# Middle elements: group statistics over DRAM in place of two small matmuls, and another order of VectorE's and ScalarE's work between the attentions

## The chip, the cores and the metric

The kernel runs on one core of one Trainium2 chip. The metric is the device time of one execution in microseconds, the median of several runs. The engines of the core have names that the text uses: TensorE (PE in the profile, its weight loads PEld) multiplies matrices into PSUM; VectorE (DVE) and ScalarE (ACT) work on SBUF and empty PSUM; GpSimd (POOL) does small things and issues some DMAs; SyncE (SP) issues most of the DMAs. Each engine works through its own queue in order.

## The reference

Two layers on x of shape (16, 256, 32, 32), in float32. With S = 1024 positions and C = 256 channels, for each of the 16 elements of the batch:

```python
# layer 0
qkv = (xs @ w_proj + b_proj).reshape(B, S, 4, 192); q, k, v = split(qkv)
attn = softmax(einsum('bihd,bjhd->bijh', q, k) * 64**-0.5, axis=2)
x = einsum('bijh,bjhd->bihd', attn, v) @ w_out + b_out + xs

# layer 1
x = x + attention(group_norm(x, gn1_w, gn1_b), qkv_w, proj_w, proj_b, phys_bias)  # 8 heads of 32
h = group_norm(x, gn2_w, gn2_b)                                                   # 32 groups of 8 channels
h = gelu(mlp_w1 @ h + mlp_b1, approximate=False)                                  # 256 -> 1024
return x + mlp_w2 @ h + mlp_b2
```

`group_norm` takes mean and variance over the 8 channels of a group and all positions, and then `(x - mean) / sqrt(var + 1e-5) * w + b`.

## The kernel before

**Tiles.** Channels lie on the 128 partitions, in two halves (`cc`); positions lie in two blocks of 512 (`t`). The two attentions keep their scores transposed: keys on partitions, 512 queries along the row. "Attention a" is that of layer 0 (4 heads of 64), "attention b" that of layer 1 (8 heads of 32). Denominators are summed on VectorE (`es`), and their reciprocals go over DRAM and back to all partitions that need them (`sp`, `row`, `d_a`, `rd_b`).

**Stages.** A loop runs over the 16 elements. For element b: attention a; then a middle stage; then attention b, into which the second half of the MLP of the element before is laced; the first half of that MLP (`hidden`: `begin`, `middle`, `finish` of four blocks i = 0 to 3) is in the middle stage. "Middle elements" are 1 to 14 (`seven` is true): there the middle stage holds, in this order on TensorE,

- the MLP's first matrix for element b - 1, as one level of Strassen's scheme: seven products per block, gathered in PSUM tiles `m`. `finish(i)` has VectorE read two PSUM halves (L1265, L1266), ScalarE apply gelu to two quarters (`gelu`, L1224), and VectorE take two differences of gelu'd quarters (`combine`, L1285);
- q and k of attention a for element b + 1, then q and k of attention b for element b, each as Winograd's seven products (`qk_by_seven`, L1096). A piece "a20" is product 2, half 0, for attention a; "b40" is product 4, half 0, for attention b. Products 1, 2, 3, 5, 6 of a half share a PSUM tile `qk_a` or `qk_b` of two banks, products 7 and 4 use the bank `qk7y`. ScalarE copies intermediate states away (L1132, L1137, L1141) and takes k out (L1116, L1118); VectorE takes q out (`leave_q`, L1122 for b, L1124 for a);
- before them VectorE makes four sums and differences of the input (`input_sums`, L1088 to L1091, tile `qk7t`), t1 to t4.

**The norm between the attentions** (`group_norm` with key `g`). `means` (L894) gets mean and variance of each channel (`mv_g`) from statistics that the output projection of attention a leaves. The mean over the eight channels of a group is then a matmul of a 128x2 operand with a constant matrix `gavg` (`averages`, tile `gm_g`), a second one gives the variance (`gv_g`); between and after them VectorE works on 128x2 tiles, GpSimd takes the power of -0.5 (L916), and four `tensor_scalar` of 128x512 (L928) write the normed tile `gn_g`.

**What sets the order.** The program is written in the order of TensorE; a scheduler keeps each engine's instructions near it. `Later` holds what is due so many pieces from now: `later.after(n, fn)`. `tc.issue_after(ins)` gives what is issued inside it a place behind the instruction `ins`, and `tc.keep_in_program_order` pins one. Before, the norm's steps are due 2 and 1 pieces after the statistics, and `input_sums` for attention b stands behind the last `finish`'s VectorE instruction (`mlp_made["added"]`), while gelus and differences stand where `finish` issues them. SP's queue carries in this stage, in this order: the reciprocals of attention a (L405, L422, L427), the load of the second MLP weights (L315) and, in the next stage, the packing of `es_b`.

PSUM is handed out in three tiles of two banks (`wide`, by least recent use) and two single banks (`bank`). A product of `qk_by_seven` that opens a tile therefore waits for the readers of what was in it; a11 opens the one that holds block 2 of the MLP before.

Of the kernel before, what the change touches and what calls it, by code (L numbers as in the profile page):

```python
# [283 lines left out]
def first_pass(ctx, tc, x, out, k):  # L284
    nc = Engines(tc)
    B, C, S = x.shape
    CC, SB, NT = C // P, S // P, S // TB
    HC = k["m1b"].shape[1]
    later = Later()

    act = ctx.enter_context(tc.tile_pool(name="act", bufs=1))
# [574 lines left out]
        return issue  # L866


    def group_norm(key, src, stats, gw, gb, tag, out_tile, wait, then=None):
        st = {}  # L870

        def averages(name, src, apart):
            if cols[0] == P:
                ps = bank(name, 1)
                product(ps[:, :CC], k["gavg"], src, start=True, stop=True)
                return [(slice(0, P), ps[:, :CC])]
            if apart:
                ps = [bank(f"{name}_{n}", n) for n in range(2)]  # L880
            else:
                both = wide(name)
                ps = [both[:, n, :] for n in range(2)]
            halves = [slice(h, h + HALF) for h in range(0, P, HALF)]
            for n, sl in enumerate(halves):
                nc.tensor.matmul(
                    ps[n][sl, :CC], k["gavg"][sl, sl], src[sl], start=True, stop=True
                )
            return [(sl, ps[n][sl, :CC]) for n, sl in enumerate(halves)]

        def means():
            mv = small.tile([P, CC, 2], F32, tag="mv", name=f"mv_{key}")
            for cc in range(CC):
                nc.vector.bn_aggr(mv[:, cc, :], stats[:, cc].rearrange("p t k -> p (t k)"))  # L894
            mean_c = small.tile([P, CC], F32, tag="mean_c", name=f"mean_c_{key}")
            nc.vector.tensor_copy(mean_c, mv[:, :, 0])
            st.update(mv=mv, mean_c=mean_c)
            later.after(wait, variances)

        def variances():  # L900
            mean = small.tile([P, CC], F32, tag="mean", name=f"mean_{key}")
            for sl, ps in averages(f"gm_{key}", st["mean_c"], True):
                nc.vector.tensor_copy(mean[sl], ps)

            dv = small.tile([P, CC], F32, tag="dv", name=f"dv_{key}")
            nc.vector.tensor_sub(dv, st["mean_c"], mean)
            nc.vector.tensor_mul(dv, dv, dv)
            nc.vector.tensor_add(dv, dv, st["mv"][:, :, 1])
            st.update(mean=mean, tv=dv)
            later.after(1 if cols[0] == P else 5, apply)  # L910

        def apply():
            rstd = small.tile([P, CC], F32, tag="rstd", name=f"rstd_{key}")
            for sl, ps in averages(f"gv_{key}", st["tv"], False):
                nc.vector.tensor_scalar(rstd[sl], ps, EPS, None, ALU.add)
            nc.gpsimd.tensor_tensor(rstd, rstd, k["mhalf"], ALU.pow)  # L916
            a = rstd
            nc.vector.tensor_mul(a, rstd, gw)
            ma = small.tile([P, CC], F32, tag="gma", name=f"gma_{key}")
            nc.vector.tensor_mul(ma, st["mean"], a)  # L920
            c = ma
            nc.vector.tensor_sub(c, gb, ma)
            y = act.tile([P, CC, S], F32, tag=tag, name=f"gn_{key}")
            out_tile.append(y)

            def part(cc, t):
                sl = slice(t * TB, (t + 1) * TB)
                nc.vector.tensor_scalar(  # L928
                    y[:, cc, sl], src[:, cc, sl],
                    a[:, cc : cc + 1], c[:, cc : cc + 1], ALU.mult, ALU.add,  # L930
                )

            if nc.in_order:
                then(y, part)
                return
            for t in range(NT):
                for cc in range(CC):
                    part(cc, t)
            if then:
                then(y)  # L940

        means()
# [140 lines left out]
    def input_sums(key, y):  # L1083
        sums = weights_tile(f"qk7t_{key}")
        b11, b12 = (y[:, 0, t * TB : (t + 1) * TB] for t in range(NT))
        b21, b22 = (y[:, 1, t * TB : (t + 1) * TB] for t in range(NT))
        t1, t2, t3, t4 = (sums[:, n] for n in range(4))
        nc.vector.tensor_sub(t3, b22, b12)  # L1088
        nc.vector.tensor_sub(t1, b12, b11)
        nc.vector.tensor_sub(t2, b22, t1)  # L1090
        nc.vector.tensor_sub(t4, b21, t2)  # L1091
        return dict(t1=t1, t2=t2, t3=t3, t4=t4, b11=b11, b21=b21, b22=b22)

    made_k = []

    def qk_by_seven(key, block, s, x, q, kk, bias=None):  # L1096
        ps, ys, got = {}, {}, []

        def aside_for():
            if not got:  # L1100
                got.append(weights_tile(f"qk7p_{key}"))
            return got[0]
# [17 lines left out]
        def leave_q(to, what, more, ch):  # L1120
            if bias is None:
                nc.vector.tensor_add(to, more, what)  # L1122
            else:
                nc.vector.scalar_tensor_tensor(  # L1124
                    to, what, bias[:, 0, ch : ch + 1], more, ALU.add, ALU.add
                )

        def p1(ch):
            both = wide(f"qk7_{key}_{ch}", order[1] if ch == 0 and bias is not None else None)
# [8 lines left out]

        def p6(ch):
            mm(ps[ch][1], s[:, ch, 1], "t2", False)  # L1140
            nc.scalar.copy(aside_for()[:, 2 * ch + 1], ps[ch][1])  # L1141

        def p2(ch):
            mm(ps[ch][0], block(1, ch, 1), "b21", False)
# [52 lines left out]
    def mlp(b, xb):  # L1197
# [61 lines left out]
        def finish(i):  # L1259
            if i == n4 - 1 and b == B - 2:  # L1260
                later.after(1, back_to_exp)
            ps = open_sums.pop(i)
            products_of(i, [(7, ps[:, 0, :], False), (6, ps[:, 1, :], False)])
            rest = gs[1, 1, i]
            nc.vector.tensor_add(unit(0, 0, i), rest, ps[:, 0, :])  # L1265
            made["added"] = nc.vector.tensor_add(rest, rest, ps[:, 1, :])  # L1266
            gelu(0, 0, i, gs[0, 0, i])
            gelu(1, 1, i, rest)
            combine((1, 0), (0, 0), False, i)
            combine((0, 1), (1, 1), False, i)  # L1270

        def back_to_exp():
            one = small.tile([P, 1], F32, tag="part", name=f"one_{b}")
# [8 lines left out]
        def combine(to, what, plus, only=None):  # L1282
            d, more = ((four if only is None else gs)[(*g, *(() if only is None else (only,)))]
                       for g in (to, what))
            (nc.vector.tensor_add if plus else nc.vector.tensor_sub)(d, d, more)  # L1285
# [179 lines left out]
    for b in range(B):  # L1465
        def load_next(b=b):
# [8 lines left out]
        later.after(14, load_next)  # L1475
        xn = []
        seven = 0 < b < B - 1
        xn_made = []
        run(
            attention_0(  # L1480
                b, tiles0, xs[b],
                lambda st, b=b, xn=xn, seven=seven, xn_made=xn_made: group_norm(
                    f"g{b}", xs[b], st, k["g1w"], k["g1b"], "res", xn, 2 if b else 1,
                    xn_made.append if seven else None,
                ),
            )
        )
# [4 lines left out]
        if seven:  # L1492
            run_pieces(hidden[:1])
            qk_parts = load_qk_blocks(b)
            run_pieces(hidden[1:2])
            with tc.issue_after(mlp_made["begun"].ins):
                sums_0 = input_sums(f"a{b}", xs[b + 1])
            made = {"a": qk_by_seven(
                f"a{b}", qk_block_0, qk_parts[:, 0], sums_0, *tiles0[:2], k["bqk"]
            )}  # L1500
            run_pieces(hidden[2:8] + [made["a"][7, 1]] + hidden[8:])
            first = first_v
        else:
            run_pieces(first[:5] if b == 0 else hidden)
# [9 lines left out]

        if seven:
            with tc.issue_after(mlp_made["added"].ins):
                sums_1 = input_sums(f"b{b}", xn_made[0])
            made["b"] = qk_by_seven(
                f"b{b}", qk_block_1, qk_parts[:, 1], sums_1, *tiles1[:2]
            )  # L1520

            def pieces(names):
                return [made[n[0]][int(n[1]), int(n[2])] for n in names.split()]

            run_pieces(pieces(
                "a10 a70 a11 a60 a40 a61 a50 a41 a51 a20 b10 a21 a30 b60 a31 b11 b70"
                " b50 b61 b71 b20"
            ))
            with tc.issue_after(made_k[-1].ins):
                mlp_made["exp"]()  # L1530
            run_pieces(pieces("b51 b40 b30 b21 b41") + v[:1] + pieces("b31"))
        else:
            aside.extend((1, 0))
            run_pieces(qk[:n] + v[:1])
# [346 lines left out]
```

## Time and profile before

| what | value |
|---|---|
| median of 3 runs | 3586.73 us (3586.65 to 3588.13) |
| the profiled execution's own time | 3587.91 us |
| its span, first to last instruction | 3586.1 us |
| mean granted TensorE clock | 1.000 |
| TensorE busy | 3573.3 us |
| VectorE busy | 2785.1 us |
| ScalarE busy | 2288.7 us |
| GpSimd busy | 220.1 us |
| middle stage of element 2, TensorE, first MLP product to first score | 494.17 to 548.30 us |
| gm_g, gv_g: matmul records in all, mean | 32 and 32, 209 and 213 ns |

A float32 matmul leaves two records in this profile. Records of TensorE overlap and their ends are modelled, so their starts are what counts. In a line of the timeline the columns are start in us from the span's start, duration, engine, line of the kernel, operation, result<-operands, shape, and how many were merged; a bracket gives the idle time ahead of it and who ended it.

### The profile page before, as it was taken

What the parts mean: (1) busy time and instruction counts of PE and PEld (TensorE: products, weight loads), DVE (VectorE), ACT (ScalarE), POOL (GpSimd) and SP (SyncE); (2) the same over time, 40 slices, a digit from 0 to 9 for tenths busy, and PEclk for the clock granted to TensorE, in tenths of its full rate; (3) what the DMA queues carried; (4) which work ended last, traced back from release to release, by engine and by line L of the source; (5) the groups of instructions that cost most, each with busy time, mean ns of one, the idle gap of its engine ahead of it and who ended that gap; (6) DMA issues with size and microseconds to landing.
All of it is one profiled execution on the core that took longest, in us unless ns stands there. A gap on an engine that the chain in (4) does not pass through costs nothing.

```text
span 3586.1 us, 82054 instructions
## 1 busy us (share of the span) xinstructions
PE 3573.3 (100%) x35713; PEld 1479.0 (41%) x35713; DVE 2785.1 (78%) x3188; ACT 2288.7 (64%) x3186; POOL 220.1 (6%) x319
## 2 busy tenths in 40 slices
PE   9999999999999999999999999999999999999999
PEld 4334344343444434444344443444434444344434
DVE  5786877868788687886868878688786877869787
ACT  5665757567575675856658566585765757657573
POOL 4000000001000010000000000000000100000000
PEclk9999999999999999999999999999999999999999
DMA  4011312213122131221312213121121211213100
GB/s 134 8 58 33 82 51 40 72 39 82 45 44 68 39 82 45 52 65 35 82 45 52 66 34 81 45 55 63 39 77 45 55 63 43 72 45 64 52 28 28
DMA packets 81606, 198.07 MB, mean 55 GB/s; under 512 B 38006, under 2 KB 38774, under 8 KB 75094
## 3 DMA queue, kind: packets, MB, share of 16 engines
q1 hardware_dynamic: 71860, 164.13, 15.0%
q0 software_dynamic: 7632, 28.21, 5.1%
q8 instruction: 282, 4.62, 0.5%
q14 instruction: 86, 0.70, 0.1%
q10 hardware_dynamic: 1746, 0.40, 0.1%
HBM read 125.59 MB, written 22.27 MB: 41 GB/s over the span
## 4 chain that ended last, share of the span: by engine, by line
PE 93%; DVE 4%; DMA 1%; issue 1%; SPq 0%; ACT 0%; DVEq 0%
PE s_b L642 13%; PE s_a L458 13%; PE acc_a L481 12%; PE acc_b L696 12%; PE m L1209 9%; PE m L381 9%; PE qk_a L1108 3%; PE qk_b L1108 3%; PE v_b L381 3%; PE j L381 3%; PE v_a L381 3%; PE o L381 3%; PE qk7y_b L1108 1%; PE qk7y_a L1108 1%; DVE es_b L670 1%
## 5 line engine op out<-in xcount | busy, mean ns | idle before, releaser
L655 ACT ACTIVATE e_b<-s_b 128x1024 f32<-128x1024 f32 (+1 forms) x1280 | 982.1, 864 | 135.3 <-PE s_b L642 135.3
L670 DVE TENSOR_TENSOR es_b<-es_b,e_b 128x2048 f32<-128x2048 f32 (+1 forms) x460 | 881.5, 1934 | 105.0 <-ACT e_b L655 88.6
L468 ACT ACTIVATE e_a<-s_a 128x1024 f32<-128x1024 f32 x512 | 521.2, 1025 | 359.1 <-PE s_a L458 356.3
L458 PE MATMUL s_a<-q,k 64*64 64x512 f32 x4096 | 544.3, 593 | 0.0
L481 PE MATMUL acc_a<-e_a,v 64*64 64x512 f32 x4096 | 540.1, 589 | 0.0
L642 PE MATMUL s_b<-q,k 32*64 32x512 f32 x8192 | 523.4, 600 | 2.7 <-ACT v L978 1.3
L495 DVE TENSOR_TENSOR es_a<-es_a,e_a 128x1024 f32<-128x1024 f32 x384 | 471.8, 1229 | 63.7 <-ACT e_a L468 42.9
L696 PE MATMUL acc_b<-e_b,v 128*32 128x512 f32 x4096 | 492.1, 598 | 0.0
L381 PE MATMUL m<-g,w 128*32 128x256 f32 (+1 forms) x6432 | 401.8, 384 | 0.0
L381 PEld LDWEIGHTS m<-g,w 128*32 128x32 f32 x6432 | 218.7, 111 | 205.0 <-issue 54.8
L481 PEld LDWEIGHTS acc_a<-e_a,v 64*64 64x64 f32 x4096 | 187.9, 133 | 251.5 <-issue 222.9
L642 PEld LDWEIGHTS s_b<-q,k 32*64 32x64 f32 x8192 | 175.8, 130 | 247.5 <-issue 122.4
L458 PEld LDWEIGHTS s_a<-q,k 64*64 64x64 f32 x4096 | 175.8, 133 | 247.0 <-issue 216.5
L696 PEld LDWEIGHTS acc_b<-e_b,v 128*32 128x32 f32 x4096 | 108.5, 109 | 351.5 <-ACT e_b L655 194.7
L1209 PE MATMUL m<-gn_h,w 128*128 128x512 f32 x504 | 238.3, 601 | 0.7 <-DVE g L1237 0.7
L670 DVE TENSOR_TENSOR es_b<-e_b,e_b 128x2048 f32<-128x2048 f32 (+1 forms) x72 | 147.0, 2051 | 105.8 <-ACT e_b L655 105.8
L1285 DVE TENSOR_TENSOR g<-g,g 128x512 f32<-128x512 f32 (+1 forms) x184 | 193.5, 1062 | 2.1 <-PE m L381 0.8
L1209 PE MATMUL m<-hs,w 128*128 128x512 f32 x380 | 176.0, 592 | 0.0
L1224 ACT ACTIVATE g<-g,m1b 128x512 f32<-128x512 f32 x128 | 91.6, 721 | 94.1 <-DVE g L1265 67.2
L1209 PEld LDWEIGHTS m<-gn_h,w 128*128 128x128 f32 x504 | 91.8, 190 | 113.9 <-issue 99.1
L1122 DVE TENSOR_TENSOR q<-qk7p_b,qk_b 128x512 f32<-128x512 f32 x28 | 19.3, 688 | 134.5 <-PE qk_b L1108 134.5
L1224 ACT ACTIVATE g<-m,m1b 128x512 f32<-128x512 f32 x128 | 81.0, 684 | 66.8 <-PE m L1209 66.8
(251 smaller groups left out, 3667.6 us busy)
## 6 DMA issues: line engine op xcount, KB each, us to landing
w<-w_kept SPq DMA_DIRECT2D x30, 1792.0 KB
packed_b<-es_b SPq DMA_DIRECT2D x42, 512.0 KB
packed_b<-es_b POOLq DMA_DIRECT2D x42, 512.0 KB, 6.3
rd_b<-row_b SPq DMA_DIRECT2D x252, 64.0 KB
out_dram<-x SPq DMA_DIRECT2D x63, 256.0 KB
d_a<-row_a SPq DMA_DIRECT2D x62, 256.0 KB
x<-in_x_dram SPq DMA_DIRECT2D x30, 512.0 KB
qk<-qk_kept SPq DMA_DIRECT2D x14, 1024.0 KB
```

The costliest lines, as they stand in the source:

```text
L381: nc.tensor.matmul(o[sl], w[:, sl], r, **flags)
L458: nc.tensor.matmul(s[h : h + HALF, g, :], kT[g * D : (g + 1) * D, c, kb * P + h : kb * P + h + HALF], qT[g * D : (g + 1) * D, c, t * TB : ...
L468: nc.scalar.activation(e, s, AF.Exp, scale=float(D) ** -0.5)
L481: nc.tensor.matmul(accs[i][h][g * D : (g + 1) * D, :], v[h * HALF : (h + 1) * HALF, kb, c * 2 + g], e[h * HALF : (h + 1) * HALF, g, :], st ...
L495: spread_out["es"] = nc.vector.tensor_add(sums[i], held[i] if kb == 1 else sums[i], e)
L642: nc.tensor.matmul(outs[g][h : h + HALF, :], kT[g * D : (g + 1) * D, c, k0 : k0 + HALF], qT[g * D : (g + 1) * D, c, t * TB : (t + 1) * TB] ...
L655: spread_out["exp"] = nc.scalar.activation(to, s, AF.Exp, scale=float(D) ** -0.5)
L670: ins = nc.vector.tensor_add(d, (d if kb else es[0][:, g : g + step]), es[m][:, g : g + step])
L696: nc.tensor.matmul(acc[g * D : (g + 1) * D, :], v[:, kb + m, c * G + g], es[m][:, g, :], start=(m == 0), stop=(m == 1),)
L1108: ins = nc.tensor.matmul(to, w, x[right], start=first, stop=True, skip_group_check=not first)
L1209: nc.tensor.matmul(ps, blocks[1][number - 1][:, i * P : (i + 1) * P], inputs[b][number], start=first, stop=True, skip_group_check=not first,)
L1285: (nc.vector.tensor_add if plus else nc.vector.tensor_sub)(d, d, more)
```

## The change

For the middle elements alone:

- The norm's averages over a group no longer come from matmuls. `mv_g` (128 partitions x 4 numbers) is written to a DRAM tile by one DMA, and a second one reads it back so that every partition has the values of all eight channels of its group (tile `of_g`, 128 x 32). `from_group` then does on VectorE: the sum of the means, their distances from the mean, squares, the variances added, the sum, and the division by eight with EPS added. It is due four pieces after the statistics.
- What both ways share after that is now `scale_by` (power, coefficients).
- The four `tensor_scalar` that write `gn_g` become a function, `all_parts`, which the main loop calls after the last `finish`, together with the input sums.
- For blocks 2 and 3 of the MLP the gelus of `finish` and the two differences are kept in lists. The gelus are issued behind ScalarE's copy of a61 (`made_got[-1]`), the differences behind VectorE's last q of attention a (`made_q[-1]`).
- t4 of the input sums is a function of its own (`sums_4`): for a it is issued at once as before, for b after the differences.

TensorE's order stays as it was except for the two matmuls that go. On VectorE, from the end of `begin`: before, coefficients, four gn, then the PSUM readers of block 2 and 3 mixed with differences, sums and the q of a; after, coefficients, the four PSUM readers, four gn, three sums, four q of a, four differences, t4.

```diff
@@ group_norm
             for cc in range(CC):
                 nc.vector.bn_aggr(mv[:, cc, :], stats[:, cc].rearrange("p t k -> p (t k)"))
+            if over_memory:
+                return around(mv)
...
+        def around(mv):
+            row = dram.tile([P // GSZ, GSZ * CC * 2], F32, tag="stats", name=f"row_{key}", bufs=2)
+            nc.sync.dma_start(row.rearrange("g (j f) -> (g j) f", j=GSZ), mv)
+            n = GSZ * CC
+            full = work.tile([P, TB], F32, tag="full", name=f"of_{key}", bufs=2)
+            nc.sync.dma_start(
+                full[:, : 2 * n], row.unsqueeze(1).to_broadcast([P // GSZ, GSZ, 2 * n])
+            )
+            later.after(wait, lambda: from_group(
+                full[:, : 2 * n].rearrange("p (j c f) -> p f c j", c=CC, f=2),
+                full[:, 2 * n : 3 * n].rearrange("p (c j) -> p c j", c=CC),
+            ))
+
+        def from_group(of_group, dv):
+            means, variances = of_group[:, 0], of_group[:, 1]
+            mean = small.tile([P, CC], F32, tag="mean", name=f"mean_{key}")
+            tc.keep_in_program_order(nc.vector.tensor_reduce(mean, means, AX.X, ALU.add))
+            nc.vector.scalar_tensor_tensor(
+                dv, mean.unsqueeze(2).to_broadcast([P, CC, GSZ]), -1.0 / GSZ, means,
+                ALU.mult, ALU.add,
+            )
+            nc.vector.tensor_mul(dv, dv, dv)
+            nc.vector.tensor_add(dv, dv, variances)
+            rstd = small.tile([P, CC], F32, tag="rstd", name=f"rstd_{key}")
+            nc.vector.tensor_reduce(rstd, dv, AX.X, ALU.add)
+            nc.vector.tensor_scalar(rstd, rstd, 1.0 / GSZ, EPS, ALU.mult, ALU.add)
+            st.update(mean=mean)
+            scale_by(rstd, 1.0 / GSZ)
...
-            for t in range(NT):
-                for cc in range(CC):
-                    part(cc, t)
+            if over_memory:
+                mlp_made["norm"] = all_parts
+                return
+            all_parts()
@@ input_sums
-        nc.vector.tensor_sub(t4, b21, t2)
+        sums_4[key] = lambda: nc.vector.tensor_sub(t4, b21, t2)
@@ finish
-            gelu(0, 0, i, gs[0, 0, i])
-            gelu(1, 1, i, rest)
-            combine((1, 0), (0, 0), False, i)
-            combine((0, 1), (1, 1), False, i)
+            steps = (
+                lambda: gelu(0, 0, i, gs[0, 0, i]),
+                lambda: gelu(1, 1, i, rest),
+                lambda: combine((1, 0), (0, 0), False, i),
+                lambda: combine((0, 1), (1, 1), False, i),
+            )
+            if 2 * i >= n4 and b + 2 < B:
+                for what, fn in zip(("gelus", "gelus", "sums", "sums"), steps):
+                    made.setdefault(what, []).append(fn)
+                return
+            for fn in steps:
+                fn()
@@ the main loop
-                    f"g{b}", xs[b], st, k["g1w"], k["g1b"], "res", xn, 2 if b else 1,
-                    xn_made.append if seven else None,
+                    f"g{b}", xs[b], st, k["g1w"], k["g1b"], "res", xn,
+                    4 if seven else 2 if b else 1, None, seven,
...
             with tc.issue_after(mlp_made["added"].ins):
-                sums_1 = input_sums(f"b{b}", xn_made[0])
+                mlp_made.pop("norm")()
+                sums_1 = input_sums(f"b{b}", xn[0])
...
-            run_pieces(pieces(
-                "a10 a70 a11 a60 a40 a61 a50 a41 a51 a20 b10 a21 a30 b60 a31 b11 b70"
-                " b50 b61 b71 b20"
-            ))
+            run_pieces(pieces("a10 a70 a11 a60 a40 a61 a50 a41 a51"))
+            with tc.issue_after(made_got[-1].ins):
+                for fn in mlp_made.pop("gelus"):
+                    fn()
+            with tc.issue_after(made_q[-1].ins):
+                for fn in mlp_made.pop("sums"):
+                    fn()
+                sums_4[f"b{b}"]()
+            run_pieces(pieces("a20 b10 a21 a30 b60 a31 b11 b70 b50 b61 b71 b20"))
```

More of the change, by code (lines that the diff above doesn't have):

```diff
@@ L288, in first_pass @@
     HC = k["m1b"].shape[1]
+    GSZ = C // GROUPS
     later = Later()
@@ L866, in out_proj, with group_norm @@
         return issue
-    def group_norm(key, src, stats, gw, gb, tag, out_tile, wait, then=None):
+    def group_norm(
+        key, src, stats, gw, gb, tag, out_tile, wait, then=None, over_memory=False
+    ):
         st = {}
@@ L915, in apply, with scale_by @@
                 nc.vector.tensor_scalar(rstd[sl], ps, EPS, None, ALU.add)
+            scale_by(rstd, None)
+        def scale_by(rstd, share):
             nc.gpsimd.tensor_tensor(rstd, rstd, k["mhalf"], ALU.pow)
@@ L919, in apply @@
             ma = small.tile([P, CC], F32, tag="gma", name=f"gma_{key}")
-            nc.vector.tensor_mul(ma, st["mean"], a)
+            if share is None:
+                nc.vector.tensor_mul(ma, st["mean"], a)
+            else:
+                nc.vector.scalar_tensor_tensor(ma, st["mean"], share, a, ALU.mult, ALU.mult)
             c = ma
@@ L924, in apply, with all_parts @@
             out_tile.append(y)
+            def all_parts():
+                for t in range(NT):
+                    for cc in range(CC):
+                        part(cc, t)
             def part(cc, t):
@@ L1090, in input_sums @@
         nc.vector.tensor_sub(t2, b22, t1)
-        nc.vector.tensor_sub(t4, b21, t2)
+        sums_4[key] = lambda: nc.vector.tensor_sub(t4, b21, t2)
         return dict(t1=t1, t2=t2, t3=t3, t4=t4, b11=b11, b21=b21, b22=b22)
-    made_k = []
+    made_k, made_q, made_got, sums_4 = [], [], [], {}
     def qk_by_seven(key, block, s, x, q, kk, bias=None):
@@ L1123, in leave_q @@
             else:
-                nc.vector.scalar_tensor_tensor(
+                made_q.append(nc.vector.scalar_tensor_tensor(
                     to, what, bias[:, 0, ch : ch + 1], more, ALU.add, ALU.add
-                )
+                ))
         def p1(ch):
@@ L1140, in p6 @@
             mm(ps[ch][1], s[:, ch, 1], "t2", False)
-            nc.scalar.copy(aside_for()[:, 2 * ch + 1], ps[ch][1])
+            made_got.append(nc.scalar.copy(aside_for()[:, 2 * ch + 1], ps[ch][1]))
         def p2(ch):
@@ L1477, in first_pass @@
         seven = 0 < b < B - 1
-        xn_made = []
         run(
@@ L1481, in first_pass @@
                 b, tiles0, xs[b],
-                lambda st, b=b, xn=xn, seven=seven, xn_made=xn_made: group_norm(
-                    f"g{b}", xs[b], st, k["g1w"], k["g1b"], "res", xn, 2 if b else 1,
-                    xn_made.append if seven else None,
+                lambda st, b=b, xn=xn, seven=seven: group_norm(
+                    f"g{b}", xs[b], st, k["g1w"], k["g1b"], "res", xn,
+                    4 if seven else 2 if b else 1, None, seven,
                 ),
@@ L1497, in first_pass @@
                 sums_0 = input_sums(f"a{b}", xs[b + 1])
+                sums_4[f"a{b}"]()
             made = {"a": qk_by_seven(
```

## The prediction

> **What bounds the kernel now.** I read the page first: busy shares, then the chain that ended last.
>
> ```profile
> PE 3573.3 (100%) x35713; PEld 1479.0 (41%) x35713; DVE 2785.1 (78%) x3188; ACT 2288.7 (64%) x3186; POOL 220.1 (6%) x319
> ...
> PE 93%; DVE 4%; DMA 1%; issue 1%; SPq 0%; ACT 0%; DVEq 0%
> ```
>
> TensorE has no idle time to speak of, and 93% of the chain is its own. But the ends of its records are modelled, so a small stall does not show as idle; it shows in the distance from one start to the next. So I went to the timeline of TensorE in the middle stage (the MLP and the making of q and k between the two attentions) of element 2:
>
> ```profile
> 514.87 1.02 PE L1209 MATMUL m<-gn_h,w 128*128 128x512 f32 x2
> 515.73 0.28 PE L381 MATMUL gm_g<-mean_c_g,gavg 128*128 128x2 f32 x2
> 515.87 1.10 PE L1209 MATMUL m<-gn_h,w 128*128 128x512 f32 x2
> 516.81 1.02 PE L1209 MATMUL m<-hs,w 128*128 128x512 f32 x2
> 517.67 0.28 PE L381 MATMUL gv_g<-dv_g,gavg 128*128 128x2 f32 x2
> 517.81 1.96 PE L1209 MATMUL m<-gn_h,w 128*128 128x512 f32 x4
> 519.61 3.60 PE L1209 MATMUL m<-hs,w 128*128 128x512 f32 x8
> ...
> 529.91 1.02 PE L1108 MATMUL qk_a<-qk7t_a,qk 128*128 128x512 f32 x2
> 530.93 1.12 PE L1108 MATMUL qk_a<-x,wp 128*128 128x512 f32 x2
> ```
>
> The pitch is to be seen: a 128x512 matmul leaves two records, and eight records from 519.61 take until 523.04, 0.429 us each. Nearly everything here starts on that pitch, so the stage is bound by TensorE, and a gain is only what breaks the pitch. Three places do, in all fourteen middle elements, alike to 0.01 us: the two matmuls of the norm, and the first product a20, which starts 1.02 us after its predecessor where two records need 0.86. Who ends that last wait is in VectorE's timeline:
>
> ```profile
> 513.53 0.20 DVE L894 BATCH_NORM_AGGREGATE mv_g<-st 128x2 f32<-128x12 f32 x1
> ...
> 517.87 0.69 DVE L1242 TENSOR_TENSOR g<-g,m 128x512 f32<-128x512 f32 x1 [1.08 <-PE m L1209]
> 518.48 0.15 DVE L915 TENSOR_SCALAR rstd_g<-gv_g 128x2 f32<-128x2 f32 x1
> 519.44 0.16 DVE L918 TENSOR_TENSOR rstd_g<-rstd_g,g1w 128x2 f32<-128x2 f32 x1 [0.81 <-POOL rstd_g L916]
> ...
> 530.13 0.75 DVE L1124 SCALAR_TENSOR_TENSOR q<-qk_a,bqk,qk7p_a 128x512 f32<-128x512 f32 x1
> ```
>
> The second L1124 ends at 530.88, a20 starts at 530.93: its PSUM tile is being read. VectorE had been busy without a break since 519.44 with gn, the MLP's differences and sums.
>
> **The change, part by part.**
>
> *The two matmuls go.* gm: 515.73 to 515.87 is 0.14 us, and the pair after it takes 0.94 to the next start instead of 0.86: 0.08 more, 0.22 together. gv: 0.14, and the four after it take 1.80 instead of 1.716: 0.22. Sum 0.45 us per element, all on TensorE's path; 14 x 0.448 = 6.3 us. They also go from a70's bank, which is then free early; a70 waited for nothing that I see.
>
> *VectorE's small work.* Removed: five 128x2 operations (L896, L903, L906 to L908) and L915, 0.2 us apart. Added: two reductions, three 128x16 operations and a 128x2 one. No 128x16 arithmetic with a broadcast is in the trace; its ends are 0.16 us (128x2) and 0.29 (the one reduction of 128x128 to 128x16). I take 0.25, the 128x16 reciprocal (0.246), and 0.28 with the gap. The chain to the end of the coefficients: 5 x 0.28 = 1.40, from L942 to the answer of GpSimd's power 0.96 (518.48 to 519.44), three small ones 0.59; 2.95 us.
>
> *The two DMAs.* Both go on SP's queue, the second waiting there for the first to land. Behind it on SP stands only the load of the second MLP weights, which before is issued at 523.24, once TensorE has left the first ones; it moves with TensorE. Nothing else of SP's comes before 574. POOL's queue keeps its order. The nearest rows are the reciprocals' way through DRAM:
>
> ```profile
> 498.49 0.32 SPq L422 DMA_DIRECT2D row_a<-inv_a  x1
> 499.89 1.10 SPq L427 DMA_DIRECT2D d_a<-row_a  x2
> ```
>
> ```profile
> 493.24 0.58 SPq L405 DMA_DIRECT2D sp_a<-d_a  x1
> ```
>
> ```profile
> 495.22 0.22 POOL L423 TENSOR_TENSOR dsum<-dsum,sp_a 128x16 f32<-128x16 f32 x1 [25.15 <-DMA sp_a<-d_a]
> ```
>
> A row of 128 small packets is in DRAM and the next issue starts 1.40 us later (1.41 to 1.55 in 26 of 32; 3.1 to 3.5 in six). A gather of 128 small packets reaches its user after 2.0 us (495.22 less 493.24). mv_g ends at 513.73, SP starts 0.04 later: 513.77 + 1.46 + 2.00 = 517.23. Against this speaks the Trainium skill, "DMA: Bandwidth & Descriptors", section "Anatomy of one DMA — SWDGE (gpsimd) path": each DMA has about 2.0 us of fixed cost, mostly the wait for the receipt of its last write, worst where HBM is the target. It is given for GpSimd's path; by it two in a row land at 517.8, estimated, not 517.2. On SP's queue here the write to DRAM is the shorter of the two, so on that point the rows differ from the page and decide. Before TensorE's shift VectorE reaches this point at 518.5: L1242 then starts at 517.87 - 0.22 = 517.65 and is followed 0.6 later, at 518.25. By row and by rule the trip is covered and the sum is the same; I take the row. The ends of the trip's price on the path are nothing and, for an access that crawls, what the third rival gives.
>
> *The order on VectorE.* From 518.25: coefficients until 521.20; then the four PSUM readers of `finish` (0.72 and 0.60 apart): 521.20, 521.92, 522.52, 523.24, so until 523.84. TensorE delivers them no later: its eighth record of `finish` ends, shifted by 0.45, at 522.8. The reader that frees the tile of a11 ends at 522.6, a11 starts at 524.76 - 0.45 = 524.3. Then four gn (1.83, as 520.03 to 521.86) until 525.67, three sums (0.60, 0.72, 0.60) until 527.59, first q until 528.25. The second q needs a50, whose last record (528.62, 0.59 long) ends shifted at 528.76: q runs 528.8 to 529.55. a20 is due at 529.91 + 0.86 - 0.45 = 530.32. So its wait goes: 0.16, and the 0.10 by which its two records are stretched after it (1.12 us where a pair takes 1.02). 0.267 x 14 = 3.7 us. Spare: 0.55 ahead of q, 0.73 behind it. With the landing's 1.02 ahead of 518.25, the trip may take 5.7 us instead of 3.46; even the slow six fit (the longest, 3.51 in place of 1.46, gives 5.5).
>
> *ScalarE.* The four gelus leave the place ahead of the copies for a60 and a61 (nothing waited; price 0) and stand behind a61's copy, which ends near 528.5; 4 x 0.65 bring them to 531.2. Behind them waits the first k, due when a20 ends at 530.32 + 0.43 + 0.59 = 531.3. Were the gelus later, a30 would wait, which is due 2.6 us after a20's start and needs only k's 0.69: 0.9 spare. The four differences and the last sum (t4 of b) come after the fourth q, about 531.3, and end near 534.7, in the hole of VectorE ahead of L1122 at 539.03 (6.84 us of waiting there); b40, which needs t4, is later. If that hole were closed they would cost 3.3 us.
>
> *What is late next.* In the stage after this TensorE keeps its pitch too: 91.34 us busy of the 91.70 us from 548.3 to 640, with VectorE at 75.57 and ScalarE at 74.07. So the shift should carry to the end.
>
> **The sum.** 14 x (0.448 + 0.267) = 10.0 us. The profiled execution took 3587.91 us, its span 3586.1 and 1.8 around it: 3577.9. The median of the runs is 1.18 us lower, 3586.73, so 3576.7 us, 0.28% faster.
>
> **The rivals.**
>
> *Only the matmuls pay.* If the operations with broadcast or the four readers take 1.3 us more than I have it, the second q is late again and a20 waits as before: 6.3 us, 3580.4. For it: every operation there was put at a mean. Against it: 1.28 us of spare.
>
> *It doesn't do what it says.* The shift is taken back later, at the weights or in the attention over memory: 3586.7. For it: VectorE is 82% busy there. Against it: TensorE's own 91.34 of 91.70; and the weights, issued in element 1 at 301.48, are first wanted at 341.2.
>
> *A wait in place of the one removed; slower.* VectorE is in order and now stands for a DMA ahead of the PSUM readers and gn. The point from which it decides: trip over 5.7 us, stall begins; over 6.3 the 0.715 are gone (a stall also stretches by 0.10); beyond 6.8 it is slower by over 0.2%. The same page, "Latency and other measured facts", has HBM's access at 0.2 us on average and 2 us at high load; 1.8 more on top of the 2.0 for each of the two, an estimate, gives 7.6: stall 1.9 + 0.1, less 0.715, times 14 is 18 us: 3605. Against it: the DMA queues are busy 7% from 494.2 to 523.0, and none of the 32 writes took over 3.51 us, no gather over 2.67.
>
> **How the numbers follow.** All of it, 3576.7: 0.70. Only the matmuls: 0.12. Given back: 0.08. The late trip: 0.10. What moves each is where the slow trips of the reciprocals fall: in three of the fourteen elements of before the stage took 1.0 to 1.5 us more (57.3, 57.7 and 57.1 us instead of 56.2, 3.6 in all), and where they fall may change. None of them gives 3573.1, two more give 3579.1: 3573 to 3579.4 for the likeliest alone. With the second case the range is 3573 to 3583, which leaves out 0.18. A measurement of this kernel tells a change from none at about 0.2%, 7.2 us: faster 0.68, within 0.22 (second and third case, and 0.02 of the first), slower 0.10.
>
> **What would show it.** Right: no gm and gv in the middle; the pair at 515.87 at 0.429 pitch; a20 0.86 after its predecessor; VectorE waiting under 0.2 us for the DMA of the group's values; ScalarE's first k not behind a gelu. Wrong: VectorE idle before the first reduction, a11 or a20 off the pitch, or a middle stage shorter by 0.7 us with the same time per element.

## The result and the profile after

| | before | after |
|---|---|---|
| median of 10 runs each | 3586.84 us (3586.51 to 3588.43) | 3577.36 us (3575.98 to 3579.74) |
| profiled execution, its span | 3587.91, 3586.1 us | 3575.98, 3574.2 us |
| middle stage where no row was slow, first to last | 56.16 us (11 of 14) | 55.45 us (11 of 14) |
| middle stage in the other three | 57.30, 57.68, 57.14 us | 56.55, 56.60, 56.64 us |

The ratio is 0.9973, with a 95% interval of 0.9964 to 0.9982: 0.27% faster, where 0.28% and 3576.7 us were predicted. The stage is measured here from the start of TensorE's last denominator record of attention a to the start of its first score of attention b. A "slow row" is one write of the reciprocals of attention a's last half to DRAM (tile `row_a`) that takes about 3 us instead of 1.5; it is shown below. Where there is none, the stage became 0.71 us shorter. The sum over all fourteen stages fell by 10.2 us, from 789.9 to 779.7. The pair of profiled executions differs by 11.9 us; the 1.7 left over lie outside the middle stages and are less than runs of one kernel differ among themselves (3.8 us over ten runs of after). The medians differ by 9.5.

The page of the changed kernel, busy shares and the chain that ended last:

```profile
PE 3561.2 (100%) x35657; PEld 1473.9 (41%) x35657; DVE 2793.3 (78%) x3188; ACT 2285.7 (64%) x3186; POOL 220.5 (6%) x319
...
PE 96%; DVE 2%; DMA 1%; issue 0%; ACT 0%; SPq 0%; DVEq 0%
```

TensorE has 56 records fewer, two matmuls of two records in each of 14 elements. VectorE is 8.2 us busier, and yet its share of the chain fell from 4% to 2%.

The timeline of TensorE in the middle stage of element 2:

```profile
513.23 1.88 PE L1255 MATMUL m<-gn_h,w 128*128 128x512 f32 x4
514.95 1.02 PE L1255 MATMUL m<-hs,w 128*128 128x512 f32 x2
515.80 1.88 PE L1255 MATMUL m<-gn_h,w 128*128 128x512 f32 x4
...
527.82 1.02 PE L1154 MATMUL qk_a<-qk7t_a,qk 128*128 128x512 f32 x2
528.68 1.02 PE L1154 MATMUL qk_a<-x,wp 128*128 128x512 f32 x2
```

The MLP's products follow each other at 0.429 us a record (four from 513.23 to 514.95 are 1.72 us), with nothing between them. a20, the last line, starts 0.86 us after its predecessor, and its pair takes 1.02 us again instead of 1.12.

VectorE's timeline of the same element, from its wait for the last sum of the MLP's second product:

```profile
516.00 0.69 DVE L1288 TENSOR_TENSOR g<-g,m 128x512 f32<-128x512 f32 x1 [1.52 <-PE m L1255]
516.61 0.17 DVE L933 TENSOR_REDUCE mean_g<-of_g 128x2 f32<-128x16 f32 x1
516.82 0.19 DVE L934 SCALAR_TENSOR_TENSOR of_g<-mean_g,of_g 128x16 f32<-128x16 f32 x1
...
518.65 0.16 DVE L955 TENSOR_TENSOR rstd_g<-rstd_g,g1w 128x2 f32<-128x2 f32 x1 [0.81 <-POOL rstd_g L953]
...
519.44 0.69 DVE L1311 TENSOR_TENSOR g<-g,m 128x512 f32<-128x512 f32 x1 [0.23 <-PE m L1255]
...
527.16 0.75 DVE L1170 SCALAR_TENSOR_TENSOR q<-qk_a,bqk,qk7p_a 128x512 f32<-128x512 f32 x1 [0.31 <-PE qk_a L1154]
...
529.55 2.49 DVE L1339 TENSOR_TENSOR g<-g,g 128x512 f32<-128x512 f32 x4
```

L933 is the first operation that needs the gathered statistics; no bracket stands behind it, so they had landed. The first PSUM reader (L1311) and the second q (L1170) now wait for TensorE, where before the second L1124 came too late for a20. That q ends at 527.91, 0.77 us ahead of a20. SyncE's two issues and ScalarE's work ahead of a30, same element:

```profile
512.12 0.33 SPq L919 DMA_DIRECT2D row_g<-mv_g  x1
513.53 0.55 SPq L922 DMA_DIRECT2D of_g<-row_g  x1
```

```profile
526.78 2.56 ACT L1270 ACTIVATE g<-g,m1b 128x512 f32<-128x512 f32 x4
529.74 0.69 ACT L1164 ACTIVATE k<-qk_a,bqk 128x512 f32<-128x512 f32 x1 [0.39 <-PE qk_a L1154]
```

The write is in DRAM 1.41 us after its issue began, when the gather can be issued. The first k waits for TensorE and not behind the four gelus.

The three elements whose stage is longer (1, 6 and 11; before 1, 7 and 13) have one slow write of the reciprocals of attention a. In the changed kernel's element 1, the issues on SyncE's queue, TensorE's starts that break the pitch because of it, and the DMA packets between the two issues (packets, MB, share of 16 engines):

```profile
274.83 0.32 SPq L423 DMA_DIRECT2D row_a<-inv_a  x1
278.08 1.11 SPq L428 DMA_DIRECT2D d_a<-row_a  x2
```

```profile
284.05 3.70 PE L382 MATMUL o<-res_a,wo 128*128 128x512 f32 x8 [0.39 <-DVE res_a L575]
...
292.21 1.98 PE L1255 MATMUL m<-gn_h,w 128*128 128x512 f32 x4 [0.17 <-DVE g L1283]
```

```profile
q1 hardware_dynamic: 144, 0.01, 3.0%
q8 instruction: 1, 0.02, 2.2%
```

The write takes 3.25 us where most take 1.4 to 1.6. Beside its 128 packets of 64 bytes (the other 16 have 4 bytes) there is one packet of 16 KB of the instruction queue, 1.19 us long, that starts just ahead of them; 120 of the 128 had ended by 275.86, and the last eight start only when it ends and have ended at 276.89. Elements 6 and 11 (writes of 3.41 and 3.29 us) show the same, again with exactly eight, which is one engine's share if the 128 are spread evenly over 16. In after and in before alike, all six of the 32 such writes that take over 2 us have a 16 KB packet in their time and eight late packets, and none of the other 26 has. The late packets do not explain all of it: from a write's last packet to the next issue it is 0.4 to 0.7 us in the quick ones, and 1.19 here. Where those 0.5 to 0.8 us more come from stays open.

### The profile page after: what moved, and what is told of

Same layout as the page of the kernel before. It is cut to its first block, busy times and chain, and to the rows that moved or that the text cites. A ratio compares the mean times of both kernels' runs of the same rounds, so it can differ in the third digit from the quotient of the medians.

```text
span 3574.2 us, 81969 instructions
## 1 busy us (share of the span) xinstructions
PE 3561.2 (100%) x35657; PEld 1473.9 (41%) x35657; DVE 2793.3 (78%) x3188; ACT 2285.7 (64%) x3186; POOL 220.5 (6%) x319
## 4 chain that ended last, share of the span: by engine, by line
PE 96%; DVE 2%; DMA 1%; issue 0%; ACT 0%; SPq 0%; DVEq 0%
PE s_b L643 14%; PE acc_b L697 13%; PE s_a L459 12%; PE acc_a L482 12%; PE m L382 10%; PE m L1255 9%; PE qk_b L1154 3%; PE qk_a L1154 3%; PE v_a L382 3%; PE v_b L382 3%; PE j L382 3%; PE o L382 3%; PE qk7y_b L1154 1%; PE qk7y_a L1154 1%; PE qk_a L382 1%; PE den_a L551 1%
## 5 line engine op out<-in xcount | busy, mean ns | idle before, releaser
L382 PE MATMUL v_a<-wp,x 128*32 128x256 f32 (+1 forms) x1952 | 121.6, 379 | 0.0
L382 PE MATMUL o<-res_a,wo 128*32 128x512 f32 (+1 forms) x640 | 118.8, 595 | 1.3 <-DVE res_a L575 1.3
```

The costliest lines, as they stand in the source:

```text
L382: nc.tensor.matmul(o[sl], w[:, sl], r, **flags)
```

## Experiments

All kernels here compute the whole reference. Where there is a ratio, the runs of the kernel before on the same chip stand beside it; otherwise one execution was made, and it is read by its stages.

### The new order alone

The norm goes by its two matmuls as before; the rest of the change stays.

```diff
-            if over_memory:
-                return around(mv)
...
-                    4 if seven else 2 if b else 1, None, seven,
+                    2 if b else 1, None, seven,
```

> The changed kernel with the old norm: the two matmuls are back, the new order of VectorE and ScalarE stays. If the parts pay as in the prediction's sum, the a20 wait stays away and gm and gv cost their 0.45 us: middle stage 0.27 us shorter than before in undisturbed elements (56.16 to 55.90), 3.7 us in all, about 3583. Rival, the order pays nothing by itself: a20 waits again (0.16 us off the pitch), stage 56.16, 3586.8.

Measured: 3583.96 us (3582.53 to 3585.31) against 3587.82, ratio 0.9989 (0.9979 to 0.9999). The stage without a slow row is 55.90 us in all eleven elements: 0.26 less than before and 0.45 more than after. TensorE's timeline of element 2 has the two matmuls and the stretched pair back, and a20 is on the pitch:

```profile
516.24 0.28 PE L382 MATMUL gm_g<-mean_c_g,gavg 128*128 128x2 f32 x2
516.38 1.10 PE L1253 MATMUL m<-gn_h,w 128*128 128x512 f32 x2
517.33 1.02 PE L1253 MATMUL m<-hs,w 128*128 128x512 f32 x2
```

So with the old norm the order is worth a20's wait (0.26 measured, 0.267 predicted) and nothing else, and in this order the two matmuls are worth 0.45 (0.448): both halves of the prediction's sum are what they were put at.

### The norm over memory alone

Gelus, differences, the four gn and t4 are issued where they were before; VectorE's PSUM readers are pinned.

```diff
-            if over_memory:
-                mlp_made["norm"] = all_parts
-                return
             all_parts()
...
+            pin = tc.keep_in_program_order if 2 * i >= n4 and b + 2 < B else (lambda ins: ins)
+            pin(nc.vector.tensor_add(unit(0, 0, i), rest, ps[:, 0, :]))
+            made["added"] = pin(nc.vector.tensor_add(rest, rest, ps[:, 1, :]))
...
-            if 2 * i >= n4 and b + 2 < B:
+            if False:
...
-                mlp_made.pop("norm")()
                 sums_1 = input_sums(f"b{b}", xn[0])
+                sums_4[f"b{b}"]()
...
-                for fn in mlp_made.pop("gelus"):
-                    fn()
...
-                for fn in mlp_made.pop("sums"):
-                    fn()
-                sums_4[f"b{b}"]()
```

> The changed kernel with the norm over memory, but gelus, differences, gn and t4 issued where they were before (the readers of PSUM pinned in their old order). Rival, the parts add up: the two matmuls go, a20 waits as before, 0.45 us per element less, 3580.5. My theory from VectorE's queue: the norm's six operations end 0.8 us later against TensorE than the old ones, and with differences and all four sums still ahead of the second q that q ends about 1.4 us after a20 is due: stall 1.4 + 0.1 in place of 0.27, so 0.8 us per element more than before, about 3598, slower than both.

Measured: 3596.33 us (3593.74 to 3598.52) against 3587.82, ratio 1.0024 (1.0014 to 1.0034). This is slower than before, although the two matmuls are gone. The stage is 56.74 us: 0.58 more than before, 1.29 more than after. The time is near that of the theory (3598; the stage was to be 0.8 longer); where the loss lies is not as the theory had it, for only a part of it is at a20. The waits of TensorE's weight loads for q and k (us in all, times, longest):

```profile
PEld qk_a L1151 <- DVE q L1167: 25.9, 28, 1.1
...
PEld qk_a L1151 <- ACT qk_a L1175: 12.8, 14, 0.9
PEld qk_a L1151 <- ACT qk7p_a L1184: 10.9, 14, 0.8
PEld qk_a L1151 <- DVE g L1310: 8.2, 14, 1.1
```

Weight loads overlap matmuls, so these times are more than the path pays; starts give that: a60 is 0.25 us late, a50 0.11, a20 0.42 and a21 0.10, and each stretches its pair by 0.10, which is 1.28 of the 1.29. Why two of them wait for ScalarE is in the timelines of element 2: VectorE's before, then VectorE's and ScalarE's in this run:

```profile
516.05 0.16 DVE L903 COPY mean_g<-gm_g 128x2 f32<-128x2 f32 x1
...
520.03 1.92 DVE L928 TENSOR_SCALAR gn_g<-x,rstd_g,gma_g 128x512 f32<-128x512 f32 x4
521.86 0.68 DVE L1265 TENSOR_TENSOR g<-g,m 128x512 f32<-128x512 f32 x1
...
523.94 0.68 DVE L1265 TENSOR_TENSOR g<-g,m 128x512 f32<-128x512 f32 x1
```

```profile
519.50 0.17 DVE L933 TENSOR_REDUCE mean_g<-of_g 128x2 f32<-128x16 f32 x1
...
522.13 1.92 DVE L973 TENSOR_SCALAR gn_g<-x,rstd_g,gma_g 128x512 f32<-128x512 f32 x4
523.96 0.68 DVE L1309 TENSOR_TENSOR g<-g,m 128x512 f32<-128x512 f32 x1
...
526.76 0.68 DVE L1309 TENSOR_TENSOR g<-g,m 128x512 f32<-128x512 f32 x1
```

```profile
524.68 1.45 ACT L1267 ACTIVATE g<-g,m1b 128x512 f32<-128x512 f32 x2 [2.80 <-DVE g L1309]
526.03 0.58 ACT L1175 COPY qk_a<-qk_a 128x512 f32<-128x512 f32 x1
```

From the last sum of the MLP's second product to the first gn is 2.63 us here; before it was 1.55 (518.48 to 520.03). The other five small operations of the old norm took no time, since VectorE did them while it had to wait anyway: one ahead of a wait of 0.48 us for ScalarE, four from 516.05 to 516.8, ahead of one of 1.08 us for TensorE. The new chain stands wholly behind that wait. So the first readers come 1.08 us later, 1.30 against TensorE, which no longer has the second matmul's 0.22 us in between; the gelus that need them come as much later, and behind the gelus in ScalarE's queue the copies that a60 and a50 wait for. In after, with the readers ahead of gn and the gelus behind the copies, none of this is left.

The run is not the memory alone to the last instruction. The order that came out differs from that of before: the third reader stands behind two differences instead of one, so it starts 2.80 us after the first instead of 2.08; the two gelus of block 3 stand next to each other, right ahead of the copies L1184; and t4 stands behind the second q instead of ahead of it. The later third reader may be what makes a50 late; t4's place takes 0.6 us of VectorE's work from ahead of the second q, for which a20 waits. So the loss is shown for this order; the memory with the order of before to the last instruction was not run.

The two parts of the change therefore do not add: the order alone took 3.9 us off, the memory alone put 8.5 us on, and both together took 9.5 off.

### The gelus back in their place

Only the differences and t4 are late; the gelus are issued by `finish`.

```diff
-                for what, fn in zip(("gelus", "gelus", "sums", "sums"), steps):
-                    made.setdefault(what, []).append(fn)
+                steps[0]()
+                steps[1]()
+                made.setdefault("sums", []).extend(steps[2:])
                 return
...
-                for fn in mlp_made.pop("gelus"):
-                    fn()
```

> The changed kernel with the four gelus of blocks 2 and 3 issued in finish as before; the differences stay late. Theory (the gelus' place is worth nothing): same stage, 55.45 us, same time, about 3577. Rival (they hold up ScalarE's copies for a60 and a61): these two start off the pitch and the stage is 0.3 us or more longer.

Measured: 3576.94 us in one execution, the stage 55.45 in eleven elements, as in after. With the readers early, moving the gelus is worth nothing.

### gn ahead of the PSUM readers

The norm over memory, gelus and differences late, but the four gn are written before the readers of `finish`, whose place is pinned.

```diff
-            if over_memory:
-                mlp_made["norm"] = all_parts
-                return
             all_parts()
...
-                mlp_made.pop("norm")()
```

> The changed kernel with the four gn operations ahead of the PSUM readers again (as before), the rest as changed. Theory (it is the differences' move that frees a20, the readers-first order is worth little): a20 on the pitch; a11 at the edge, its tile's last reader ends at about the moment its weights would be loaded: 0 to 0.25 us per element, 3577 to 3581. Rival (emptying PSUM first is what pays): a20 or a11 off the pitch by 0.5 us or more, 3584 or above.

Measured: 3578.74 us in one execution. The stage is 55.45 us in ten elements and 55.57 in one; the three with a slow row have 57.82, 57.14 and 56.66, and in the first two of these a11 waits for VectorE, by 0.85 and 0.19 us. So "PSUM first", too, is worth almost nothing in a quiet element once the differences are out of the way; what it does is to leave slack where an element is disturbed. One execution does not tell how often. That leaves the late differences and t4 as what frees a20; they were not put back by themselves, and gelus and gn were not put back together.

### One, two and three more hops through DRAM

To lengthen the trip without touching anything else, the row of statistics is copied on within DRAM; VectorE's operations of the norm and its readers are pinned, and its order is that of after. The edit is that of one hop; the others have `range(2)` and `range(3)`.

```diff
+            for hop in range(1):
+                src_row = row
+                row = dram.tile([P // GSZ, GSZ * CC * 2], F32, tag=f"hop{hop}", name=f"hop{hop}_{key}", bufs=2)
+                nc.sync.dma_start(row, src_row)
```

> The changed kernel with one more DMA in the norm's way (DRAM to DRAM, 2 KB), VectorE's order pinned as it is. A trip of about 5.2 us instead of 3.5. Prediction's spare (stall from 5.7 on): no stall, stage 55.45 us, VectorE idle 0.5 to 1 us ahead of the norm's first reduction. Rival (the trip was only just covered): a20 off the pitch by about the added 1.5 to 2 us, 20 us in all.

> Two more DMAs in the way, a trip of about 7 us. By the prediction's spare a20 stalls by 7 - 5.7 = 1.3 us and 0.1 after it: stage about 56.8 us in undisturbed elements, some 19 us more than the changed kernel, so slower than the kernel before. Rival (more spare than I have): stage near 55.45.

> Three more DMAs, a trip of about 8.7 us: every further us goes straight to TensorE, so the stage grows by what one more hop takes (1.5 to 1.8 us) over the run with two: 58.4 us, some 42 us more than the changed kernel. Rival (a late norm is taken up by another gap): grows by less than 1 us.

*One hop:* 3579.63 us in one execution. From SyncE's start of the write to the first reduction it is 5.5 to 6.5 us. VectorE now stands for the DMA in every element:

```profile
DVE mean_g L937 <- DMA of_g<-hop_g: 20.5, 14, 2.0
```

In elements without a slow row its 0.98 to 1.56 us of standing cost nothing: the stage stays 55.45. With 1.60 us it is 55.49, with 1.74 (trip 6.31) 55.55, with 1.92 (trip 6.49) 55.74; a20 is what is late there, in the last case by its old 0.16 and 0.10, with 0.03 at a11. The spare is about 1.57 us of VectorE, reached at a trip of about 6.1 us.

*Two hops:* 3597.77 us in one execution, slower than before. Trips are 7.3 to 8.2 us, stages 56.6 to 57.5 (58.3 to 58.6 with a slow row). Waits, and then TensorE's timeline in element 2 (columns as above):

```profile
DVE mean_g L937 <- DMA of_g<-hop_g: 44.5, 14, 3.8
PEld qk_a L1160 <- DVE g L1319: 25.8, 14, 2.5
```

```profile
526.05 1.13 PE L1160 MATMUL qk_a<-x,wp 128*128 128x512 f32 x2 [0.65 <-DVE g L1319]
```

The larger stall is now a11's, which opens the PSUM tile of block 2 and waits for its reader (its start is 0.8 to 1.8 us late, and 0.10 goes to the stretched pair). a20 pays the old 0.16 and 0.10 and no more, since TensorE itself has been moved back.

*Three hops:* 3737.53 us in one execution, where about 3619 was expected; the stages are 66.6 to 68.8 us. The cause is another than the hop. SyncE's queue and VectorE's first reduction, element 1:

```profile
295.71 2.27 SPq L923 DMA_DIRECT2D hop_g<-hop_g  x2
300.21 0.33 SPq L316 DMA_DIRECT2D w<-w_kept  x1
300.60 0.57 SPq L926 DMA_DIRECT2D of_g<-hop_g  x1
```

```profile
307.53 0.18 DVE L937 TENSOR_REDUCE mean_g<-of_g 128x2 f32<-128x16 f32 x1 [11.77 <-DMA of_g<-hop_g]
```

The load of the second MLP weights (1792 KB) was now ordered ahead of the gather. The 16 KB of the gather reach their user 6.9 us after their issue, where they took 2.02 in the one element of after in which VectorE waited for them. Then TensorE, which had stood for 9.61 us, runs at a lower clock. Stretches of element 1 (stretch, length, busy time of PE, PEld, DVE, ACT and POOL, granted clock, DMA share, GB/s):

```profile
301.90:304.70 2.80, 0.00 (x1) 0.00 (x0) 0.00 (x0) 0.59 (x1) 0.00 (x0) 1.00 0.87 353
304.80:311.50 6.70, 0.00 (x0) 0.00 (x0) 2.88 (x12) 0.00 (x0) 0.70 (x1) 0.50 0.22 90
311.50:314.90 3.40, 3.39 (x4) 1.51 (x5) 3.37 (x7) 0.57 (x1) 0.00 (x0) 0.50 0.00 0
315.00:336.60 21.60, 21.60 (x55) 10.07 (x54) 10.78 (x17) 13.10 (x21) 0.00 (x0) 1.00 0.00 0
```

The granted clock falls to 0.50 when TensorE has stood for 2.8 us and stays there until it has worked for 3.5 us again; in that time its records start 0.80 to 1.01 us apart instead of 0.43. This run says nothing of a trip that is three hops long, but it shows what SyncE's order is worth: the change's gather stands ahead of that load, in every element.

### The reciprocals of attention a earlier

What is left over the pitch in after are the three slow rows. Here the reciprocals of attention a's last half are no longer pinned, so that VectorE makes them 2.4 us earlier, and the output projection after them is due one piece later.

```diff
-            tc.keep_in_program_order(nc.vector.reciprocal(inverse, spread))
+            made = nc.vector.reciprocal(inverse, spread)
+            if not early:
+                tc.keep_in_program_order(made)
...
+                lambda full: scale(t, full), early=t == NT - 1 and b > 0,
...
-                later.after(3 if b else 4, lambda: project(t, res)())
+                later.after(4, lambda: project(t, res)())
```

> The changed kernel with the reciprocals of attention a's last half let free on VectorE, so that they run 2.4 us earlier, ahead of the MLP's first VectorE work. Theory: in three elements of fourteen the output projection waits 1.1 us for the reciprocals' way through DRAM when a write to DRAM takes 3.2 us instead of 1.4; with 2.4 us more this wait goes: all fourteen stages at 55.45 us, about 3574. Rival (the wait has another cause, or the later statistics hold up the norm): three or more stages stay 1.1 us longer, or all get longer; 3577 or above.

Measured: 3573.91 us (3573.41 to 3575.01) against 3587.03, ratio 0.9964 (0.9950 to 0.9977): 3.4 us below after, faster than both kernels. All fourteen stages are 55.48 or 55.49 us. SyncE's queue in element 1:

```profile
273.03 0.32 SPq L425 DMA_DIRECT2D row_a<-inv_a  x1
274.55 1.11 SPq L430 DMA_DIRECT2D d_a<-row_a  x2
```

The write is no longer slow: in none of the fourteen middle stages did it take over 1.57 us, and none has a 16 KB packet of the instruction queue in its time. So in this execution the two transfers merely no longer meet. Whether a slow one would now be covered, as the expectation had it, the run does not tell, and the edits were not tried one by one.

## Why the prediction was right

The result was 3577.4 for 3576.7, and its reasons held in the profile and under experiment. By its own steps:

- **The two matmuls, 0.448 us an element:** shown. After against the order alone differs by 0.45 us in each undisturbed stage.
- **a20's wait, 0.267:** shown, by 0.26 for the order alone and by a20's place on the pitch in after.
- **Which sum:** the addition of the two is right for the change as a whole and wrong as an account of its parts. The prediction priced the longer chain on VectorE inside the new order and found it covered. It did not say that the first half of the gain depends on that order. Without it the memory trip cost 8.5 us, in the order that run had. The case "only the matmuls pay" at 3580.4 supposed that the worst thing VectorE could do was to bring a20's old wait back. The run of the memory alone shows a wait that is larger (0.42 instead of 0.16) and three more, two of them through ScalarE.
- **Small operations on VectorE:** the kind was right, the size not. The 128x16 operations take 0.17 to 0.19 us and start 0.21 apart, where 0.28 was taken; from the first reduction to the end of the coefficients (516.61 to 519.20) the chain is 2.6 us instead of 2.95. It went into waits for TensorE (0.23 at the first reader), so the path did not see it.
- **The trip:** the write is 1.40 to 1.44 us in nine elements, as the profile's row said (1.46), but 2.0 to 2.5 in the other five, though their packets had all ended 1.02 us after the issue as in the nine (why the next issue came later stays open); the gather is 2.02 us in the one element where VectorE waits for it, for 0.13 us. The rule weighed against the row, about 2.0 us of fixed cost for each DMA (the Trainium skill, "DMA: Bandwidth & Descriptors", "Anatomy of one DMA — SWDGE (gpsimd) path", given there for GpSimd's path), is too much for the quick writes and about right for the gather. The trip's size made no difference, since the spare covered both.
- **The spare:** 1.28 us was worked out, about 1.57 measured with one hop; the trip may last 6.1 us instead of 5.7, 0.3 more, which is what the shorter chain gives. Break-even lies between a trip of 6.5 us (0.29 of the 0.71 us gone) and one of 7.4 (a stage of 56.63, more than all of it gone); 6.3 was predicted.
- **The slower rival:** its mechanism exists and reaches the other side of before, with two hops. Two things in it were off. It put 3605 us at a trip of 7.6; by the larger spare, trips of 7.3 to 8.2 gave 3597.8. And only the margin is a20's, as the rival had it; from there on a11 takes the whole growth, because it waits for a PSUM reader that stands directly behind the coefficients, and moves everything after it.
- **Gelus at no price:** right in the changed kernel (k waits 0.39 us for TensorE, and with the gelus back nothing changes). The cover to be named was the readers' early place: where the readers are late and the gelus stand ahead of the copies, they hold them up, and that cost a60 and a50 0.57 us an element (0.25, 0.11 and two stretched pairs) in the run of the memory alone. With late readers and late gelus (the run with gn ahead of the readers) it cost nothing in ten of eleven undisturbed elements.
- **Differences and t4 in VectorE's hole:** they end at 532.64, and VectorE then waits 4.04 us for TensorE; covered.
- **Given back later:** no. The stages' 10.2 us are in the total: 11.9 in the profiled pair, 9.5 by the medians.
- **Slow rows:** three of fourteen before, three after, worth 3.6 and 3.4 us. The prediction's number took three for granted and said so; nothing in it told that it would stay three, so that part of the agreement is luck. They are no chance of a single execution: the traces with the old norm have them in elements 1, 7 and 13, those with the new one in 1, 6 and 11, and the run with the earlier reciprocals in none. That they are a meeting with the instruction queue is read from the packets; it was not forced by an experiment.

## What to carry to other kernels

Where one engine sets the pace at an even pitch, a change is worth the places that break the pitch and no more; but a part that is free in the whole change can cost more than the whole gains when it is made alone, so price each part in the order of work it will really stand in. Small operations that an engine does while it waits for another are free, and as many on the far side of that wait make the chain longer. When a trip through DRAM is put ahead of work in an engine's queue, work out how long the engine may stand before the first reader behind it is late, and see that no large transfer can get ahead on the same queue.

## What the runs showed of the hardware

- A small write of 128 packets was held up when one 16 KB packet of the instruction queue ran among them: 120 packets had ended within 1.0 us of the issue, the last eight 1.0 us later, and the issue behind the write came after 3.25 us instead of 1.4, of which the packets explain only those 1.0.
- A 16 KB gather issued 0.4 us behind a 1792 KB load on the same queue reached its user after 6.9 us instead of 2.0.
- TensorE idle for 9.6 us came back with a granted clock of 0.50, which had fallen 2.8 us into the pause and was 1.00 again after 3.5 us of work; that the clock falls when idle and needs some microseconds of work is what the Trainium skill says ("TensorE: Matmul & The Clock Gate", "Part 1: The HAM clock gate"), and the pauses of up to 1.8 us at a11 with two hops left the granted clock at 1.0.
- Each wait of a product of 0.1 us or more named above (a60, a50, a20, a21 and a11, at the clock of 1.0) also stretched the pair behind it by 0.10 us, from 0.86 to 0.96 between starts.
